# Adding x by a GpSimd transfer instead of VectorE, with GpSimd in the recorded order and a margin on ScalarE

## The chip, the cores and the metric

The kernel runs on one core of a Trainium2 chip. The metric is the device time of one execution in microseconds (us). Before the change the median of three runs is 2365.49 us (2364.38 to 2368.03).

The engines go by the profile's names: PE is TensorE's matrix multiplication and PEld its weight load, DVE is VectorE, ACT is ScalarE, POOL is GpSimd, SP is the engine that issues most transfers. Each runs its own queue of instructions in order; semaphores tie them together.

## The reference

Two graph layers on x (64 samples of 256 nodes by 256 features), both with the same matrix `adj` (256 by 256) and a residual:

```python
def reference(x, adj, L0_W1, L0_W2, L0_W3, L1_W1, L1_b1, L1_W2, L1_b2):
    # layer 0
    G = adj * adj
    h = maximum(layernorm(x), 0)
    h = relu(G @ (h @ W1)); h = relu(G @ (h @ W2))   # 256 -> 512 -> 1024
    x = x + G @ (h @ W3)                             # 1024 -> 256
    # layer 1
    h = maximum(layernorm(x), 0)
    U = eigenvectors of the normalized Laplacian of adj (jnp.linalg.eigh)
    x = x + U @ (relu((U.T @ h) @ W1 + b1) @ W2 + b2)
```

Layer 0 needs only `adj`. Layer 1 needs the eigenvectors, which are found on the chip.

## The kernel before

**Two kinds of work beside each other.** The class `Eigen` finds U in one long chain of dependent small steps: 254 Householder steps (`tridiagonalize`), small blocks (`leaves`), four levels of merging (`level`, 32 to 256), and two last products (`vectors`, `join`). VectorE does most of it; TensorE gives short transposes and products, ScalarE squares and roots, GpSimd powers and one-element steps. The class `Layers` does the two layers on 32 pairs of samples. Each pair's tiles have 128 partitions: [P, H, 2, N] is 128 partitions by two halves of the nodes by two samples by 256 features, 512 KB in f32.

**The order.** `Pace` puts both into one program. The chain's instructions are issued as they are written (`Pace.chain`). Each `Op` has an estimated busy time, and `Pace` keeps a clock for each engine and for each tile. Before it issues an instruction of the chain, `run` issues instructions of the streams (the layers' work) for as long as `fits` says that they can be done before the chain's is due. An instruction that is due sits at `ready` plus `LATER` (0.4 us for TensorE, 0.1 us for ScalarE). Ahead of a chain instruction on TensorE a stream's instruction need only start before that (0.5 us later for ScalarE's); ahead of one on another engine a stream's TensorE or ScalarE instruction has to end before it, and a stream's instruction of the remaining engines need only start. Large products can be cut at the limit (`Op.cut`). Until U is done, `manual_schedule` (L2352) keeps the recorded order for TensorE and ScalarE; the order of VectorE, GpSimd and SP in that stretch comes from the library's own scheduler. In the layer-1 stretch (`layer1`) all engines keep the recorded order.

**The streams.** `products` (L1905) holds the matrix work of layer 0. In the round of pair q it does the third product of q (`third_by_seven`, seven products for eight; its ScalarE copies and two adding transfers from GpSimd, `add`, fill tile s2), in it the rows of the pair before (`last(q - 1)`), then the first product and the widening of pair q+1, `rectify`, then `turn_rows` (transposes of the normalized rows of pair q-1 on TensorE), `fourth`, and `for_layer1(q - 1)`, which forms hw and spills it to DRAM. `rows` (L1950) holds the norms: `begin(q + 2)` loads x and normalizes it for layer 0, then, when `last(q)` is done (`q in self.new`), `norm1(q)` normalizes x1 in place for layer 1. `turn_rows` waits until `norm1` has been issued.

**x1.** There is one tile `x1`. Before, `products` loads x of pair q into it by two transfers on SP, after `for_layer1(q - 1)` has read the tile for the last time. In `last(q)` TensorE forms G p3 in a PSUM bank, for m = 0 and 1, and VectorE adds the bank onto x1 (128x512 each). After m = 1 the tile is spilled to DRAM by SP for layer 1's residual, and `norm1` begins: four sums and four squares on ScalarE (`norm`), three small steps on GpSimd (v, scale by a power, shift), four relu on ScalarE (`relu_norm`).

**The chain's ScalarE and GpSimd steps.** In a Householder step of the first half (lo < 128) `below` squares and sums the new row xr on ScalarE (tile tail, shown as m) and copies one element on GpSimd; `length` forms nn on VectorE, its root s0 by a power on GpSimd and the sign q on GpSimd. nb (shown as m<-q,s) needs s0 and q. The tile none on GpSimd needs tail and nn and is read by den. The transposes of ac and of a column of A (psB, psA) are TensorE's part. In the second half the root is ScalarE's. In `level` the roots rdq and the powers zh and rn are GpSimd's.

In the profile nearly every instruction has line L208, that of the recorder's call; tiles tell them apart: x<-x,bank is the add onto x1, bank<-eye,x is `turn_rows`, bank<-p,gt is `last`, bank<-hw,u and bank<-ut,s belong to layer 1, psA<-q,m is a chain product at the end of a level.

Of the kernel before, what the change touches and what calls it, by code (L numbers as in the profile page):

```python
# [21 lines left out]
F32 = mybir.dt.float32  # L22
AF = mybir.ActivationFunctionType
OP = mybir.AluOpType
# [135 lines left out]
class Pace:  # L160
# [9 lines left out]
    LEAD = 1.5  # L170

    def __init__(self, nc):
        self.slower, self.lead, self.no_haste = self.SLOWER, 0.0, False
        self.now = Proxy(nc, self.chain)
        self.later = Proxy(nc, lambda op: op)
        self.clock = dict.fromkeys(ENGINES.values(), 0.0)
        self.written, self.read, self.streams, self.on = {}, {}, [], True
# [32 lines left out]
    def chain(self, op):  # L210
        if not self.on:
            return op.call(*op.args, **op.kwargs)
        due = self.ready(op) + self.LATER.get(op.engine, 0.0)
        if self.no_haste:
            due = max(due, self.clock[op.engine] + 0.01)
        self.run(due, None if self.no_haste else op.engine)
        return self.issue(op, self.slower)

    def fits(self, op, start, limit, engine):
        if engine is None or op.engine not in ("PE", "ACT"):  # L220
            return start < limit
        if engine == "PE":
            return start < limit + self.HOP * (op.engine == "ACT")
        return start + op.busy + self.lead * (op.engine == "ACT") < limit
# [55 lines left out]
class Eigen:  # L280
# [162 lines left out]
    def tridiagonalize(self, a):  # L443
# [63 lines left out]
        for k in range(N - 2):  # L507
            lo = k + 1
            r, rest = slice(lo, N), slice(lo + 1, N)
            halves = [0, 1] if lo < P else [1]  # L510
            hs = slice(halves[0], H)
            rc = a[:, :, lo]

            nb = nbs[:, k : k + 1]
            if qn is not None:
                rs, qs = self.col("rs", 1), self.col("qs", 1)
                self.recip(rs, s0)
                self.tt(qs, q, s0, OP.mult)
            xa, junk = self.col("xa"), self.row("r0")
            for h in halves:  # L520
                self.stt(junk[:, r], a[:, h, r], 1.0, xr[:, r], OP.mult, OP.mult, accum=xa[:, h : h + 1])
                if h == halves[0] and qn is not None:
                    self.stt(nb, rs, qn, qs, OP.mult, OP.add)
            if qn is None:
                self.stt(nb, q, 2.0, s0, OP.mult, OP.mult)

            ac, uc = self.col("ac"), us[:, :, k]
            self.stt(ac[:, hs], rc[:, hs], nb, xa[:, hs], OP.mult, OP.add)
            pu, pr = as_row("psB", ac, halves), as_row("psA", rc, halves)

            none = self.col("none", 1)
            nc.gpsimd.tensor_scalar(none, tail, 1e-30, 1e30, OP.is_le, OP.mult)
            nc.gpsimd.tensor_tensor(none, none, nn, OP.add)
            den, gg, gu = (self.col(c, 1) for c in ("den", "gg", "gu"))
            gam = gams[:, k : k + 1]
            u1 = xr[:, lo : lo + 1]
            self.tt(u1, u1, nb, OP.add)
            self.stt(den, alpha, nb, none, OP.mult, OP.add)
            self.recip(gam, den)
            self.stt(uc, ident[:, :, lo], nb, xc, OP.mult, OP.add)  # L540
            aside(lo).tensor_tensor(gg, gam, gam, OP.mult)
            aside(lo).tensor_tensor(gu, gg, u1, OP.mult)
            gc, gr = self.col("gc"), row("gr")
            if halves[0]:
                self.tt(gc[:, hs], ac[:, hs], gam, OP.mult)
            else:
                self.ts(gc, ac, gam, OP.mult)

            uau, c = self.col("uau", 1), self.col("c", 1)
            self.stt(junk[:, r], pu[:, r], 1.0, xr[:, r], OP.mult, OP.mult, accum=uau)  # L550
            self.ts(gr[:, r], pu[:, r], gam, OP.mult)

            xn, xcn, both, f = row("xr"), self.col("xc"), self.row("r1"), self.col("f", 1)
            self.stt(both[:, rest], gr[:, rest], u1, pr[:, rest], OP.mult, OP.subtract)
            self.stt(f, uau, gu, gr[:, lo : lo + 1], OP.mult, OP.subtract)
            self.stt(xn[:, rest], xr[:, rest], f, both[:, rest], OP.mult, OP.subtract)
            more = lo + 1 < N - 1
            if more:
                alpha1, tail1 = below(xn, lo + 1)
            self.stt(c, uau, 0.5, gg, OP.mult, OP.mult)  # L560
            wr, wc = row("wr"), self.col("wc")
            self.stt(wr[:, r], xr[:, r], c, gr[:, r], OP.mult, OP.subtract)
            self.stt(wc[:, hs], uc[:, hs], c, gc[:, hs], OP.mult, OP.subtract)
            if more and halves[0]:
                following = length(xn, lo + 1, tail1)
            if halves[0]:
                nc.gpsimd.memset(xcn[:, 0:1], 0.0)
            self.stt(xcn[:, hs], gc[:, hs], u1, rc[:, hs], OP.mult, OP.subtract)
            self.stt(xcn[:, hs], uc[:, hs], f, xcn[:, hs], OP.mult, OP.subtract)
            aside(lo).tensor_tensor(xcn[:, hs], xcn[:, hs], self.lower[:, hs, lo], OP.mult)  # L570
            if more and not halves[0]:
                following = length(xn, lo + 1, tail1)

            for h in halves:
                self.stt(a[:, h, r], wr[:, r], uc[:, h : h + 1], a[:, h, r], OP.mult, OP.add)
                self.stt(a[:, h, r], xr[:, r], wc[:, h : h + 1], a[:, h, r], OP.mult, OP.add)
            xr, xc = xn, xcn
            if more:
                alpha, tail, (nn, s0, q, qn) = alpha1, tail1, following

        done = slice(0, N - 2)
        e0 = self.row("r1")[:, done]
        self.tt(e0, nbs[:, done], alphas[:, done], OP.add)
# [1186 lines left out]
class Layers:  # L1770
# [46 lines left out]

    def load(self, q):
        self.x = x = self.io.tile([P, H, 2, N], F32, tag="x", name="x")
        rows = self.view(self.ap["x"], q)  # L1820
        for i in range(2):
            at = (slice(None), slice(None), i) if q == 0 else (slice(None), i)
            yield self.nc.sync.dma_start(out=x[at], in_=rows[at])
# [81 lines left out]
    def products(self):  # L1905
# [3 lines left out]
        for q in range(PAIRS):  # L1909
            more, seven = q + 1 < PAIRS, q >= SEVEN_FROM  # L1910
            if q == SEVEN_FROM:
                yield from self.fold_weights()
            last = self.last(q - 1) if q > 0 else iter(())
            for part in self.third_by_seven() if seven else self.third():
                if part is None:
                    yield from next(last, ())
                else:
                    yield part
            if more:
                yield from self.first(q + 1)  # L1920
                for b in range(2):
                    yield from self.widened(b)
            if seven:
                yield from self.rectify(0)
            forms = iter(())
            if more:
                forms = self.spread_by_seven() if q + 1 >= SEVEN_FROM else self.spread_in_turn()
            if q > 0:
                yield lambda: q - 1 in self.h1
                yield from self.turn_rows()  # L1930
            yield from next(forms, ())
            if seven:
                yield from self.rectify(1)
            products = self.fourth()
            yield from next(products)
            if q > 0:
                yield from self.for_layer1(q - 1)
            for i in range(2):
                yield self.nc.sync.dma_start(out=self.x1[:, i], in_=self.view(self.ap["x"], q)[:, i])
            for part in products:  # L1940
                yield from next(forms, ())
                yield from part
# [7 lines left out]
    def rows(self):  # L1950

        yield from self.begin(0)
        for q in range(PAIRS):
            for p in [1, 2] if q == 0 else [q + 2]:
                if p < PAIRS:
                    yield lambda: p - 1 in self.begun
                    yield from self.begin(p)
            yield lambda: q in self.new
            yield from self.norm1(q)

    def begin(self, q):
# [219 lines left out]
    def last(self, q):  # L2181

        nc, x1 = self.nc, self.x1
        def rows(m):
# [1 line left out]
            yield from self.products_of(  # L2186
                ps, [(self.gt2[:, h, m * P : (m + 1) * P], self.p3[:, h, :]) for h in range(H)]
            )
            yield nc.vector.tensor_tensor(flat(x1)[:, m, :], flat(x1)[:, m, :], ps, OP.add)
            if m == H - 1:  # L2190
                yield nc.sync.dma_start(out=self.spilled[q], in_=x1.rearrange("p h b f -> p (h b f)"))
                self.new.add(q)

        for m in range(H):
# [138 lines left out]
def tile_kernel(ctx: ExitStack, tc: tile.TileContext, ap):  # L2333
# [5 lines left out]
    with ExitStack() as inner:  # L2339
# [9 lines left out]

        layers.nc, layers.now = pace.later, pace.now  # L2350
        pace.streams = layers.streams()
        with tc.manual_schedule(engines={mybir.EngineType.PE, mybir.EngineType.Activation}):  # L2352
            eigen.vectors(u, ut)
            pace.go_on(FLAG_US)
        pace.on = False
# [37 lines left out]
```

## Time and profile before

| what | value |
|---|---|
| median of the runs | 2365.49 us |
| the profiled execution, its own time | 2369.36 us |
| its span | 2367.6 us |
| TensorE idle in the span (span less busy) | 77.4 us |
| VectorE, x<-x,bank | 64 instructions, 43.4 us |
| ScalarE busy | 1183.8 us |
| GpSimd busy | 698.7 us |
| loads of x by SP (into x and into x1) | 128 transfers of 256 KB, 3.0 us to landing |
| adding transfers by GpSimd | 93 of 768 KB, 5.8 to 5.9 us to landing |

A line of the page's groups reads: line, engine, operation, out<-in by tile names, shape, count; then busy time in all and mean ns of one; then idle time of the engine before these and what ended it. A line of the waits reads: engine, what it was about to write, what it waited for, then us in all, times, the longest. A line of a timeline reads: start and duration in us, engine, line, operation, out<-in, count, and in brackets the idle time before and its releaser; equal neighbours are merged. A line of the stretches gives the window, its length, the busy time of PE, PEld, DVE, ACT and POOL with counts, the clock granted to TensorE as a share of full speed, the share of the transfer engines, and GB/s. A 128x256 product in f32 is two instructions in the profile.

### The profile page before, as it was taken

The numbers are of one execution on the slowest core, as the hardware profiler recorded it, in microseconds if no ns is written. First come the engines' busy times: TensorE is split into PE (matmuls) and PEld (weight loads), VectorE is DVE, ScalarE is ACT, GpSimd is POOL, SyncE is SP. The second block draws the span as 40 slices with busy tenths as digits, with TensorE's granted clock in tenths as the row PEclk, the third lists the DMA queues.
The fourth block names the chain that finished last, engine by engine and source line by source line (L and its number), as shares of the span: only waits on it lengthen the run. The fifth ranks groups of instructions, "written<-read, shape, count | busy, mean of one in ns | idle before, by whom it ended". The sixth has DMA issues, their size and how long they took to land. (4 is left out here: it accounts for less than half of the span.)

```text
span 2367.6 us, 40804 instructions
## 1 busy us (share of the span) xinstructions
PE 2290.2 (97%) x10652; PEld 1854.7 (78%) x10652; DVE 2005.0 (85%) x12072; ACT 1183.8 (50%) x2951; POOL 698.7 (30%) x1946
## 2 busy tenths in 40 slices
PE   7999999999999999999999899999999999999999
PEld 4687878787777877787888788777778777887888
DVE  7999999999999999999999899999877687882343
ACT  4455554555555555555555345555554455543322
POOL 3444544445554222222222001111111111111443
PEclk9999999999999999999999999999999999999999
DMA  4022222122222222222222222322322222223675
GB/s 134 23 70 61 65 57 70 51 69 63 59 59 62 72 56 61 69 67 59 72 63 60 58 63 72 72 72 59 72 63 63 59 58 72 54 63 103 217 251 203
DMA packets 91359, 183.26 MB, mean 77 GB/s; under 512 B 8432, under 2 KB 61808, under 8 KB 91120
## 3 DMA queue, kind: packets, MB, share of 16 engines
q0 software_dynamic: 13392, 73.14, 15.6%
q1 hardware_dynamic: 77728, 107.45, 13.4%
q8 instruction: 86, 1.41, 0.2%
q14 instruction: 153, 1.25, 0.2%
HBM read 65.48 MB, written 41.94 MB: 45 GB/s over the span
## 5 line engine op out<-in xcount | busy, mean ns | idle before, releaser
L208 PE MATMUL bank<-forms,L_gnn_W 128*128 128x256 f32 (+2 forms) x2102 | 490.7, 382 | 9.2 <-DVE x L208 6.1
L208 PE MATMUL bank<-L_gnn_W,s 128*128 128x256 f32 x2086 | 476.0, 378 | 4.8 <-ACT s L208 4.7
L208 PEld LDWEIGHTS bank<-forms,L_gnn_W 128*128 128x128 f32 x2102 | 390.6, 191 | 73.3 <-issue 11.7
L208 PEld LDWEIGHTS bank<-L_gnn_W,s 128*128 128x128 f32 x2086 | 391.7, 192 | 57.3 <-ACT s L208 5.7
L208 ACT ACTIVATE s<-bank 128x512 f32<-128x512 f32 (+1 forms) x485 | 278.7, 579 | 174.3 <-PE bank L208 173.3
L208 PE MATMUL bank<-forms,sums 128*128 128x256 f32 (+1 forms) x1512 | 347.0, 377 | 0.0
L208 PEld LDWEIGHTS bank<-forms,sums 128*128 128x128 f32 x1512 | 283.3, 191 | 53.4 <-issue 15.5
L208 PE MATMUL bank<-gt,s 128*128 128x256 f32 (+1 forms) x1036 | 246.3, 377 | 1.1 <-ACT s L208 1.1
L208 PE MATMUL bank<-L_gnn_W,y 128*128 128x512 f32 (+3 forms) x538 | 230.8, 572 | 1.1 <-ACT y L208 1.1
L208 ACT ACTIVATE forms<-bank 128x512 f32<-128x512 f32 x217 | 128.9, 594 | 180.9 <-PE bank L208 180.7
L208 PEld LDWEIGHTS bank<-gt,s 128*128 128x128 f32 x1036 | 188.9, 190 | 24.8 <-ACT s L208 2.6
L208 POOL COPY m<-xr 128x1 f32<-128x1 f32 x254 | 59.9, 236 | 418.1 <-DVE xr L208 418.0
L208 PEld LDWEIGHTS bank<-L_gnn_W,y 128*128 128x128 f32 x538 | 98.7, 190 | 98.2 <-issue 87.3
L208 ACT ACTIVATE junk<-xr 128x254 f32<-128x254 f32 (+63 forms) x127 | 46.0, 362 | 200.5 <-DVE xr L208 200.4
L208 ACT ACTIVATE junk<-x 128x256 f32<-128x256 f32 x256 | 105.8, 413 | 71.9 <-issue 44.0
L208 DVE SCALAR_TENSOR_TENSOR A<-xr,wc,A 128x255 f32<-128x255 f32 (+63 forms) x381 | 139.2, 368 | 0.0
L208 DVE SCALAR_TENSOR_TENSOR A<-wr,q,A 128x255 f32<-128x255 f32 (+63 forms) x381 | 138.0, 365 | 0.0
L208 ACT ACTIVATE junk<-x,nm 128x256 f32<-128x256 f32 x256 | 128.7, 503 | 4.0
L208 PE MATMUL bank<-p,gt 128*128 128x512 f32 (+2 forms) x272 | 122.8, 567 | 0.0
L208 PE MATMUL bank<-gt,h 128*128 128x256 f32 (+1 forms) x520 | 119.1, 379 | 0.1
L208 DVE SCALAR_TENSOR_TENSOR r<-A,xr 128x255 f32<-128x255 f32 (+63 forms) x381 | 117.8, 309 | 0.2
L208 PE MATMUL psB<-ident,ac 128*128 128x128 f32 x381 | 84.7, 277 | 27.2 <-DVE z L208 15.0
(614 smaller groups left out, 4639.5 us busy)
## 6 DMA issues: line engine op xcount, KB each, us to landing
x<-in_x_dram SPq DMA_DIRECT2D x128, 256.0 KB, 3.0
x<-x SPq DMA_DIRECT2D x64, 512.0 KB, 3.5
forms<-forms POOLq DMA_DIRECT2D x31, 768.0 KB, 5.8
s<-s POOLq DMA_DIRECT2D x31, 768.0 KB, 5.9
s<-forms POOLq DMA_DIRECT2D x31, 768.0 KB, 5.8
hw<-hw SPq DMA_DIRECT2D x64, 256.0 KB, 3.1
out_dram<-out SPq DMA_DIRECT2D x64, 256.0 KB, 2.2
L_gnn_W<-in_L_gnn_W_dram SPq DMA_DIRECT2D x1, 2048.0 KB, 11.2
```

Of the source, the lines that this page charges most:

```text
L208: return op.call(*op.args, **op.kwargs)
```

## The change

1. `Pace` gets `late`, which is added to the due time of the chain's ScalarE instructions. `tridiagonalize` sets it to 0.5 us in the steps of the first half and 0.2 us in those of the second, and to 0 after them.
2. `fits` has a rule for GpSimd: ahead of a GpSimd instruction of the chain, a stream's GpSimd instruction goes only when it ends before the limit. `manual_schedule` now covers GpSimd as well, so its queue keeps the recorded order until U is done.
3. `last` copies the bank into x1 by ScalarE. The two loads of x into x1 go. In `rows`, before `norm1`, GpSimd issues a transfer that adds x from DRAM onto x1 (512 KB), and the spill by SP follows it there.
4. The host lays x out by tile, [pair, partition, half, sample, feature], so that a partition's part of a pair is contiguous in DRAM. `load` reads it in this form.

```diff
@@ -170,7 +170,7 @@
     LEAD = 1.5
 
     def __init__(self, nc):
-        self.slower, self.lead, self.no_haste = self.SLOWER, 0.0, False
+        self.slower, self.lead, self.no_haste, self.late = self.SLOWER, 0.0, False, 0.0
         self.now = Proxy(nc, self.chain)
         self.later = Proxy(nc, lambda op: op)
         self.clock = dict.fromkeys(ENGINES.values(), 0.0)
@@ -210,13 +210,15 @@
     def chain(self, op):
         if not self.on:
             return op.call(*op.args, **op.kwargs)
-        due = self.ready(op) + self.LATER.get(op.engine, 0.0)
+        due = self.ready(op) + self.LATER.get(op.engine, 0.0) + self.late * (op.engine == "ACT")
         if self.no_haste:
             due = max(due, self.clock[op.engine] + 0.01)
         self.run(due, None if self.no_haste else op.engine)
         return self.issue(op, self.slower)
 
     def fits(self, op, start, limit, engine):
+        if engine == "POOL" == op.engine:
+            return start + op.busy < limit
         if engine is None or op.engine not in ("PE", "ACT"):
             return start < limit
         if engine == "PE":
@@ -509,6 +511,7 @@
             r, rest = slice(lo, N), slice(lo + 1, N)
             halves = [0, 1] if lo < P else [1]
             hs = slice(halves[0], H)
+            self.pace.late = 0.5 if lo < P else 0.2
             rc = a[:, :, lo]
 
             nb = nbs[:, k : k + 1]
@@ -578,6 +581,7 @@
             if more:
                 alpha, tail, (nn, s0, q, qn) = alpha1, tail1, following
 
+        self.pace.late = 0.0
         done = slice(0, N - 2)
         e0 = self.row("r1")[:, done]
         self.tt(e0, nbs[:, done], alphas[:, done], OP.add)
@@ -1817,7 +1821,7 @@
 
     def load(self, q):
         self.x = x = self.io.tile([P, H, 2, N], F32, tag="x", name="x")
-        rows = self.view(self.ap["x"], q)
+        rows = self.ap["x"][q]
         for i in range(2):
             at = (slice(None), slice(None), i) if q == 0 else (slice(None), i)
             yield self.nc.sync.dma_start(out=x[at], in_=rows[at])
@@ -1935,8 +1939,6 @@
             yield from next(products)
             if q > 0:
                 yield from self.for_layer1(q - 1)
-            for i in range(2):
-                yield self.nc.sync.dma_start(out=self.x1[:, i], in_=self.view(self.ap["x"], q)[:, i])
             for part in products:
                 yield from next(forms, ())
                 yield from part
@@ -1956,6 +1958,8 @@
                     yield lambda: p - 1 in self.begun
                     yield from self.begin(p)
             yield lambda: q in self.new
+            yield self.nc.gpsimd.dma_start(out=self.x1, in_=self.ap["x"][q], accum_op=OP.add)
+            yield self.nc.sync.dma_start(out=self.spilled[q], in_=self.x1.rearrange("p h b f -> p (h b f)"))
             yield from self.norm1(q)
 
     def begin(self, q):
@@ -2186,9 +2190,8 @@
             yield from self.products_of(
                 ps, [(self.gt2[:, h, m * P : (m + 1) * P], self.p3[:, h, :]) for h in range(H)]
             )
-            yield nc.vector.tensor_tensor(flat(x1)[:, m, :], flat(x1)[:, m, :], ps, OP.add)
+            yield nc.scalar.copy(flat(x1)[:, m, :], ps)
             if m == H - 1:
-                yield nc.sync.dma_start(out=self.spilled[q], in_=x1.rearrange("p h b f -> p (h b f)"))
                 self.new.add(q)
 
         for m in range(H):
@@ -2349,7 +2352,7 @@
 
         layers.nc, layers.now = pace.later, pace.now
         pace.streams = layers.streams()
-        with tc.manual_schedule(engines={mybir.EngineType.PE, mybir.EngineType.Activation}):
+        with tc.manual_schedule(engines={mybir.EngineType.PE, mybir.EngineType.Activation, mybir.EngineType.Pool}):
             eigen.vectors(u, ut)
             pace.go_on(FLAG_US)
         pace.on = False
@@ -2378,6 +2381,7 @@
 
     nc = bacc.Bacc("TRN2", target_bir_lowering=False, num_devices=1)
     data = {name: np.ascontiguousarray(inputs[name]) for name in INS}
+    data["x"] = data["x"].reshape(PAIRS, 2, H, P, N).transpose(0, 3, 2, 1, 4).copy()
     data.update(constants())
     arrays, ap = {}, {}
     for name, a in data.items():
@@ -2385,7 +2389,7 @@
         ap[name] = nc.dram_tensor(
             f"in_{name}_dram", a.shape, mybir.dt.from_np(a.dtype), kind="ExternalInput"
         ).ap()
-    ap["out"] = nc.dram_tensor("out_0_dram", data["x"].shape, F32, kind="ExternalOutput").ap()
+    ap["out"] = nc.dram_tensor("out_0_dram", inputs["x"].shape, F32, kind="ExternalOutput").ap()
     with tile.TileContext(nc) as tc:
         tile_kernel(tc, ap)
     r = run_bass_kernel_spmd(nc, [arrays], core_ids=[0])
```

## The prediction

> **What bounds the kernel now.** I read the page first, then the waits of TensorE, then the stretches and timelines in which it stood still.
>
> ```profile
> span 2367.6 us, 40804 instructions
> PE 2290.2 (97%) x10652; PEld 1854.7 (78%) x10652; DVE 2005.0 (85%) x12072; ACT 1183.8 (50%) x2951; POOL 698.7 (30%) x1946
> ```
>
> TensorE is the bound: 2290.2 of 2367.6 us busy, so 77.4 us of idle time. The eigenvalue chain (mostly VectorE) runs beside the layers until about 2178 us and takes small slots of TensorE. A faster chain alone therefore gains nothing; only time in which TensorE stands still, or runs slowly, can be won. The waits of TensorE name it:
>
> ```profile
> PE psB L208 <- DVE z L208: 15.0, 19, 1.9
> PE psB L208 <- DVE xr L208: 10.6, 12, 1.7
> PE bank L208 <- ACT s L208: 8.6, 6, 3.8
> ...
> PE bank L208 <- DVE x L208: 6.1, 5, 3.6
> PE psA L208 <- DVE m L208: 4.8, 1, 4.8
> ```
>
> The first two are the tridiagonalization (transposes that came before the chain was ready), the others single stalls later. Two of those, at the chain's end:
>
> ```profile
> 2152.49 1.04 PE L208 MATMUL bank<-eye,x 128*128 128x128 f32 x8
> 2158.35 3.78 PE L208 MATMUL psA<-q,m 128*128 128x256 f32 x8 [4.82 <-DVE m L208]
> 2161.93 4.46 PE L208 MATMUL bank<-L_gnn_W,s 128*128 128x256 f32 x14
> ...
> 2194.39 3.02 PE L208 MATMUL bank<-ut,s 128*128 128x256 f32 x8 [2.80 <-ACT s L208]
> ```
>
> A stall costs more than its idle time. In dense stretches 16 of the 128x256 instructions start within 3.46 us (2149.03 to 2152.49), 0.216 us each. After the 4.82 us of idle time the next 22 took from 2158.35 to 2166.22, 7.87 us instead of 22 x 0.216 = 4.75: 3.1 us more. The stretches show why: the granted clock.
>
> ```profile
> 2158.00:2162.00 4.00, 3.65 (x9) 2.93 (x10) 0.69 (x2) 1.06 (x1) 0.00 (x0) 0.50 0.16 32
> 2162.00:2166.00 4.00, 4.00 (x14) 3.29 (x13) 0.88 (x2) 1.47 (x5) 0.70 (x1) 0.69 0.00 0
> ```
>
> (The last three figures are clock, DMA share and GB/s.) The same dip, 0.50 and then about 0.7, follows the stalls at 1769.61 (3.76 us), 1878.49 (3.61 us) and 2194.39 (2.80 us). I price each at 3.1 us on top of the stall. The Trainium skill (TensorE: Matmul & The Clock Gate, Part 1) halves the clock only after an idle window of about 3.4 us and for about 3.4 us. By it the 2.80 us stall would be free of a dip and the other three would cost some 1.7 us each, 5.1 us in all, an estimate; the rows give four dips and 12.4 us, and I go by the rows.
>
> **The adds leave VectorE.** Removed are 64 adds from PSUM; added are 64 ScalarE copies and 32 adding transfers issued by GpSimd.
>
> ```profile
> L208 DVE TENSOR_TENSOR x<-x,bank 128x512 f32<-128x512 f32 x64 | 43.4, 680 | 19.2 <-PE bank L208 19.2
> L208 ACT COPY x<-bank 128x512 f32<-128x512 f32 x64 | 34.4, 579 | 2.4 <-PE bank L208 2.3
> ```
>
> VectorE loses 43.4 us of work and 19.2 us of standing before a bank. ScalarE gains 64 x 0.579 = 37 us on an engine half idle. For TensorE the direct effect is that a bank is emptied by a short copy and not by an add behind the chain's instructions: the 6.1 us of waits for "DVE x" go, and the dip after the 3.61 us one: 6.1 + 3.1 = **-9.2 us**. Cover gone would mean the same wait for the copy instead (+9 us). I add **+1** for 64 more bank releases by ScalarE.
>
> **The path of x1.** Before, the last normalized rows (relu) stood 8.6 to 11.9 us after the second add, and in all but the last two pairs TensorE turned them only 24 to 32 us after the add. Now the copy (0.58) is followed by an issue on GpSimd (the existing adding transfers take 0.97 us on the queue) and a landing; 768 KB of that kind land in 5.8 to 5.9 us. 512 KB aren't in the trace: between the 3.0 us of a plain 256 KB load and 5.9 us; I take 5.9, the same kind. The path grows by 0.58 + 0.97 + 5.9 - 0.68 = 6.8 us, to 15.4 to 18.7 us, inside the 24 us. It costs nothing, hidden by the rest of the third product, the first product and the widening of the next pair; without that cover it would be 6.8 us a pair. The spill waits for the landing and must be read before the relu overwrites x1, but means, squares and GpSimd's three steps (at least 6 us) still lie between; on SP's queue only later loads and spills of hw stand behind it, a pair (66 us) ahead. SP also loses 64 loads into x1, which nobody waited for. The layout by tile turns 1 KB runs into 2 KB on loads hidden anyway. The Trainium skill (SBUF — State Buffer, SBUF: two separate sides) speaks against a transfer issued by GpSimd beside a busy VectorE: from 0.62 to 3.1 us in its example, an estimated 2.5 us a pair. The 31 transfers of tile s here landed in 5.7 to 6.9 us with VectorE 94% busy, and 2.5 us more would still be hidden.
>
> **Tridiagonalization (50 to 1310 us).** Here 36 of the adds lay in VectorE's chain: 36 x 0.68 = 24.5 us, and one 4.1 us wait. Against it stands ScalarE's margin of 0.5 us (first half of the steps) and 0.2 us. In the trace the chain's Square begins within 0.094 us of its row in 124 of 127 steps, and VectorE's nn starts 0.033 us after the total: no slack, so a filler in the way delays VectorE in full. Bounds: 0 and 127 x 0.5 + 127 x 0.2 = 89 us. ScalarE is about 55% busy, so I take half the steps, delayed by half the margin: 127 x 0.125 + 127 x 0.05 = 22 us. GpSimd now has its power before the sign and "none": s0 ends about 0.5 us sooner, but nb also needs the sign (0.46 us), so nothing is won or lost. The chain gains 28.6 - 22 = 6.6 us. The built programs' orders agree: priced at 0.432 us per 256-column product, step 240 stands behind 1277.9 us of TensorE work instead of 1285.1. Chain and order move together, so the waits stay: **0**, between -15 (most of the 24 us idle here) and +22 (the delay is double).
>
> **GpSimd by the clock.** The queue's order now comes from the recorder. What that mends is this:
>
> ```profile
> 1764.14 0.72 POOL L208 TENSOR_TENSOR rdq<-rdq,half 128x2 f32<-128x2 f32 x1 [4.36 <-DVE rdq L208]
> ...
> 1766.30 0.20 POOL L208 TENSOR_TENSOR shift<-nm,scale 128x4 f32<-128x4 f32 x1
> ```
>
> The layers' norm waited behind a root of the chain that waited 4.36 us for VectorE; ScalarE's relu waited for the shift, its rectification for the relu, TensorE 3.76 us for that, plus the dip. I credit this 3.8 + 3.1 and the two smaller "ACT s" waits after 1400 us with 0.9 + 0.3, at seven in ten: **-6 us**; such meetings may also arise anew (bounds -8 and +7). At the start the power of the degrees no longer stands behind the norm's three (11.89 us, ready at 10.70): **-1 us**.
>
> **The chain's end.** Total matrix work is the same: 5957 instead of 5960 products in the built program. But the last product of the chain stands behind 2169.3 us of TensorE work instead of 2187.5. So 18 us of layer 0 are left to lie beside the chain's last waits and the first layer-1 pairs: between the transposes of the last level and psA<-q,m there are now some 10.5 us of products instead of 5.2. Idle there was 4.8 + 2.8 + 0.5 + 0.5 = 8.6 us and two dips 6.2: 14.8. The last pair keeps a short path: 31 products, 13.4 us, between its second copy and its turning, against 15.4: 2 us. **-12 us**, bounds -14.8 and -4.
>
> Sum: -9.2 + 1 + 0 - 6 - 1 - 12 = -27; I keep 2 us for new meetings on ScalarE: **-25 us**, a span of 2343 for 2367.6. The profiled execution itself took 2369.4 us, 3.9 above the median of 2365.5; the same difference on the median gives **2341 us**.
>
> **Rivals.** (A) The gain is given back: the margin delays the chain by 40 us rather than 22 while the order expects 22, so the transposes wait some 18 us more, and one dip stays: 2341 + 21 = 2362. For it: nn has no slack. Against: the order contains the margin already. (B) Slower: GpSimd's queue blocks the chain. Each adding transfer waits in order for a ScalarE copy; the chain's power, sign and "none" stand behind it, and psB with them. It decides from a lateness of 0.15 us in each of 254 steps, 38 us: 2341 + 38 = 2379. For it: "m" on VectorE already follows the power by 0.033 us in the median. Against: only 20 pairs meet that half, and the new rule lets in only GpSimd work that ends before the chain's is due. (C) The waits of the tridiagonalization fall too, by 15 to 20 us: 2324. For it: VectorE loses its 4.1 us stall and GpSimd's collisions (12.9 us of "m" waiting for s).
>
> **Numbers.** Forecast 0.68 (own range 2330 to 2355), C 0.14, A 0.09, B 0.09. A measurement here tells some 0.2% (4.7 us) from no change. Faster: forecast and C, 0.82; within: A, 0.09; slower: B, 0.09. The range 2320 to 2364 leaves out B, half of A and a little of C.
>
> **What would show it.** Right: "DVE x" gone from TensorE's waits; psB waits near 25 us; no dip at 1880 and 2160; the last chain product some 18 to 25 us sooner; ScalarE busy about 1220 us, VectorE 1960. Wrong: TensorE waiting for "ACT x" at the turning of rows in every pair (the landing is not hidden), or psB waits over 45 us (A or B), with VectorE waiting for GpSimd's s, q or none if it is B.

## The result, and the profile after

The changed kernel takes 2385.2 us (median of 4 runs, 2384.4 to 2386.5) against 2366.4 us for the kernel before (2364.4 to 2368.0). The ratio is 1.008, with a 95% interval of 1.0063 to 1.0098: slower. The forecast was 2341 us and its range ended at 2364: the time moved the other way.

The head of the page after, from the profiled execution:

```profile
span 2384.7 us, 40670 instructions
PE 2292.4 (96%) x10646; PEld 1850.6 (78%) x10646; DVE 1975.8 (83%) x12008; ACT 1227.1 (51%) x3015; POOL 723.7 (30%) x1978
```

TensorE is as busy as before to 2 us and the span is 17.1 us longer, so TensorE still bounds the kernel and stands idle for longer. VectorE has 29 us less work, and the kernel gained nothing by it. The waits of TensorE after (total us, number, longest):

```profile
PE psB L208 <- DVE z L208: 32.8, 31, 3.2
PE psB L208 <- DVE xr L208: 20.1, 29, 1.6
PE bank L208 <- ACT s L208: 5.6, 5, 4.4
...
PE bank L208 <- DMA hw<-hw: 3.9, 1, 3.9
```

"DVE x" is gone, as the change meant. But the two psB rows, the transposes of the tridiagonalization that find their operand not ready, went from 25.6 us in 31 waits to 52.9 us in 60. What VectorE waited for in that stage shows why. Between 50 and 1310 us, before:

```profile
DVE r L208 <- PE psB L208: 22.3, 74, 1.0
DVE m L208 <- POOL s L208: 10.0, 30, 1.1
...
DVE den L208 <- POOL none L208: 3.6, 12, 0.6
```

and after:

```profile
DVE r L208 <- PE psB L208: 36.3, 58, 3.6
DVE den L208 <- POOL none L208: 34.0, 50, 1.9
DVE m L208 <- POOL q L208: 9.7, 16, 1.7
DVE nn L208 <- ACT junk L208: 2.1, 6, 0.8
```

The new wait is den's, for GpSimd's none: 3.6 us became 34.0 us. ScalarE's margin, which the prediction counted as a cost, shows in the last row as 2.1 us of waiting. One such step (n = 153) in the timeline after. GpSimd:

```profile
649.55 0.38 POOL L208 COPY m<-xr 128x1 f32<-128x1 f32 x1
649.90 0.55 POOL L208 TENSOR_TENSOR xc<-xc,lower 128x2 f32<-128x2 f32 x1
650.41 1.20 POOL L208 TENSOR_TENSOR scale<-v,rsqrt 128x4 f32<-128x4 f32 x1
651.59 0.53 POOL L208 TENSOR_TENSOR s<-nn,half 128x1 f32<-128x1 f32 x1
652.10 0.22 POOL L208 TENSOR_SCALAR q<-xr 128x1 f32<-128x1 f32 x1
652.30 0.19 POOL L208 TENSOR_TENSOR shift<-nm,scale 128x4 f32<-128x4 f32 x1
652.57 0.27 POOL L208 TENSOR_SCALAR none<-m 128x1 f32<-128x1 f32 x1
652.92 0.19 POOL L208 TENSOR_TENSOR none<-none,nn 128x1 f32<-128x1 f32 x1
```

and VectorE in the same step:

```profile
652.35 0.16 DVE L208 SCALAR_TENSOR_TENSOR m<-q,s 128x1 f32<-128x1 f32 x1 [1.65 <-POOL q L208]
...
653.14 0.22 DVE L208 SCALAR_TENSOR_TENSOR den<-m,none 128x1 f32<-128x1 f32 x1 [0.40 <-POOL none L208]
```

and TensorE:

```profile
649.66 1.04 PE L208 MATMUL bank<-eye,x 128*128 128x128 f32 x8
653.64 0.40 PE L208 MATMUL psB<-ident,ac 128*128 128x128 f32 x2 [2.95 <-DVE z L208]
```

VectorE's nn was ready at 649.6 us, but GpSimd took the layers' scale (1.20 us) ahead of the power s, and their shift between the sign q and none. VectorE stood 1.65 + 0.40 us, z came late, and TensorE, whose order is fixed, stood 2.95 us before the transpose. Layers' work (the norm's v, scale and shift, and the issues of transfers) stands between the copy of alpha and the none pair in 65 of 254 steps after, in 5 before. In the recorded program none comes late in a step, behind nb, ac and as_row, and the streams of the layers are recorded up to there as GpSimd's planned clock allows. The library's scheduler, which ordered GpSimd before, had almost always put none ahead of them. Between 50 and 1310 us den waits 41.8 us for none in the changed kernel, the waits too short for the view included: 15.9 us in steps with operations of the norm alone in between, 17.2 us in steps with the issue of a transfer, 8.8 us in steps with no layers' work there.

**One account for all kernels.** Take each TensorE product's start minus the start before it, less its dense pitch in the trace (216 ns for 256 columns, 429 for 512, 110 for 128, 323 for 384): the rest is time lost, idle or at a halved clock. In all 14 kernels of this study the span less that loss is 2264.4 to 2264.9 us. So every difference below is time that TensorE lost, and the place can be told: until the last row (xr) of the tridiagonalization, in the leaves and levels until the first product with the vectors (hw,u), and behind it. "Ahead" is the TensorE work that stands in the queue before that last row: the row's time less the loss until then (some 4.5 us of start-up are in it).

```
kernel                            time   lost: tridiag. levels end   last row  ahead
before                          2366.4           51.9   43.4   7.5   1299.7   1247.8
after                           2385.2           89.6   20.7   9.9   1330.9   1241.3
e1 GpSimd by library            2367.4           58.3   36.3   8.5   1299.6   1241.3
e2 no margin                    2395.3           91.6   28.5  11.8   1318.7   1227.1
e3 before, GpSimd by clock      2394.7           90.6   33.2   5.8   1338.1   1247.5
e4 none recorded early          2372.7           62.6   33.2  10.9   1293.3   1230.7
e5 x1 alone                     2384.9           65.9   42.3  12.0   1292.9   1227.0
e6 margin alone                 2377.2           61.7   40.7   8.7   1313.9   1252.2
e7 by clock behind only         2352.2           54.5   20.8   8.5   1295.8   1241.3
e8 e7 without margin            2372.4           65.4   27.7  12.4   1292.4   1227.0
e9 before, by clock behind only 2357.6           51.7   33.8   5.6   1299.2   1247.5
e10 e7, half margin             2369.0           58.0   32.8  11.1   1288.4   1230.4
e11 e5, copy on VectorE         2371.6           56.1   43.8   3.0   1303.7   1247.6
e12 e7, 1.5 x margin            2350.3           51.5   26.2   4.7   1310.9   1259.4
```

(us; times are medians, all else is from one profiled execution of each kernel. Beside e1 to e12 the kernel before took 2365.7 to 2367.5 us.) Up to the last row e1 and e7 run the same sequence on all five queues and still differ by 3.8 us, so differences of that size tell nothing. From before to after, the tridiagonalization lost 37.7 us and the levels won 22.7.

### The profile page after: what moved, and what is told of

Its sections match the earlier page's. It is cut to its first block, busy times and chain, and to the rows that moved or that the text cites. A ratio compares the mean times of both kernels' runs of the same rounds, so it can differ in the third digit from the quotient of the medians.

```text
span 2384.7 us, 40670 instructions
## 1 busy us (share of the span) xinstructions
PE 2292.4 (96%) x10646; PEld 1850.6 (78%) x10646; DVE 1975.8 (83%) x12008; ACT 1227.1 (51%) x3015; POOL 723.7 (30%) x1978
## 3 DMA queue, kind: packets, MB, share of 16 engines
q1 hardware_dynamic: 52384, 90.67, 10.9%
## 5 line engine op out<-in xcount | busy, mean ns | idle before, releaser
L208 PE MATMUL bank<-forms,L_gnn_W 128*128 128x256 f32 (+1 forms) x2098 | 489.0, 381 | 0.8 <-DVE ac L208 0.8
L208 PE MATMUL bank<-L_gnn_W,s 128*128 128x256 f32 (+1 forms) x2076 | 474.1, 378 | 5.3 <-ACT s L208 5.2
L208 PEld LDWEIGHTS bank<-gt,s 128*128 128x128 f32 x1046 | 193.9, 193 | 25.5 <-ACT s L208 1.8
L208 PE MATMUL psB<-ident,ac 128*128 128x128 f32 x381 | 85.9, 280 | 55.1 <-DVE z L208 32.8
L208 PEld LDWEIGHTS psB<-ident,ac 128*128 128x128 f32 x381 | 46.5, 136 | 109.4 <-issue 59.3
L208 PE MATMUL bank<-p,gt 128*128 128x512 f32 (+3 forms) x268 | 122.7, 573 | 0.0
L208 PE MATMUL bank<-gt,h 128*128 128x256 f32 x514 | 118.3, 380 | 0.0
```

## The experiments

**e1: GpSimd back to the library's order, the rest of the change kept.**

```diff
-with tc.manual_schedule(engines={PE, Activation, Pool}):
+with tc.manual_schedule(engines={PE, Activation}):
```

> The changed kernel with GpSimd's order left to the library's scheduler again, as it was before; margin, copy, adding transfer and layout stay. Theory 'late none': with GpSimd issued in the recorded order, work of the layers stands between a step's alpha and its none, because none is recorded last in the step; den waits for none, the chain slides, TensorE waits for psB. It expects 2340 us (2330 to 2350), VectorE's den waiting under 5 us for none (41.8 us in the changed kernel), TensorE's waits for psB released by z and xr near 25 us. Rival 'margin': the ScalarE margin makes nn wait; expects 2380 us (2370 to 2390), psB waits still over 45 us. Rival 'blocked queue': the adding transfer on GpSimd's queue waits for the copy and holds up the chain behind it; expects 2370 to 2385 us.

Measured: 2367.4 us, ratio 1.0004 (0.9994 to 1.0014). VectorE's waits between 50 and 1310 us:

```profile
DVE r L208 <- PE psB L208: 25.0, 64, 4.0
DVE m L208 <- POOL s L208: 13.7, 34, 1.8
DVE den L208 <- POOL none L208: 5.8, 10, 1.4
DVE nn L208 <- ACT junk L208: 4.7, 8, 1.0
```

den's wait falls to 5.8 us, and the psB waits to 30.4 us. The margin stayed and den's wait went: "margin" falls as the cause of the slowdown. But the time is that of before, not 2340: copy, transfer and margin together are worth nothing here, and the order of GpSimd had also won something in the levels (20.7 us lost with it, 36.3 without). Up to the last row TensorE, ScalarE and SP run the same sequence in e1 as in the changed kernel. GpSimd's differs, and VectorE's with it (1093 of 7548 places), since the library orders VectorE. What is measured here as the price of GpSimd's order includes this.

**e2: no margin.**

```diff
-self.pace.late = 0.5 if lo < P else 0.2
+self.pace.late = 0.0
```

> The changed kernel with the ScalarE margin set to 0 in all steps; GpSimd issued in the recorded order, copy, adding transfer and layout stay. Theory 'late none': 2385 us (2379 to 2391), den still waiting over 30 us for none. Rival 'margin': 2345 us (2335 to 2360). Rival 'blocked queue': 2385 us.

Measured: 2395.3 us, ratio 1.0117 (1.01 to 1.0134); den waits 36.4 us between 50 and 1310 us. Without the margin the kernel is 10 us slower, outside the interval of every theory, and the opposite of what "margin" says. The last row comes 12.2 us sooner, but 14.2 us less TensorE work stands ahead of it, and the levels lose 7.8 us more.

**e3: the kernel before, with nothing but GpSimd by the clock.**

```diff
-with tc.manual_schedule(engines={PE, Activation}):
+with tc.manual_schedule(engines={PE, Activation, Pool}):
...
 def fits(self, op, start, limit, engine):
+    if engine == "POOL" == op.engine:
+        return start + op.busy < limit
```

> The kernel before with only GpSimd issued in the recorded order by the planner's clock; x1 is still added by VectorE and loaded by SP, no margin. Theory 'late none': slower than before, 2400 us (2390 to 2415), den waiting 30 us or more for none. Rivals 'margin' and 'blocked queue', which need the margin or the adding transfer: 2366 us, den waiting for none as little as before (4 us).

Measured: 2394.7 us, ratio 1.0113 (1.0096 to 1.013), as "late none" expected. Between 50 and 1310 us:

```profile
DVE den L208 <- POOL none L208: 39.4, 53, 2.3
DVE r L208 <- PE psB L208: 25.5, 46, 2.0
```

The whole loss of the tridiagonalization is there (90.6 us against 89.6 after), without a copy on ScalarE, an adding transfer or a margin: GpSimd's order is the cause of it. The new rule in `fits` alone is not: e1 keeps it and loses 58.3 us. The rival "blocked queue" falls too, as far as it means the transfer of x (only 7 of the 65 steps have one ahead of none). The older adding transfers stand in GpSimd's queue in e3 as well, and their part isn't told apart from the norm's.

**e4: none recorded early.** All three parts of the change stay; the sign is recorded right behind alpha, the first none operation ahead of nn, the second behind the power.

```diff
 nc.gpsimd.tensor_copy(alpha, xr[:, lo : lo + 1])
+q = self.col("q", 1)
+if lo < P:
+    nc.gpsimd.tensor_scalar(q, xr[:, lo : lo + 1], 0.0, 0.5, OP.is_ge, OP.subtract)
...
+nc.gpsimd.tensor_scalar(none, tail, 1e-30, 1e30, OP.is_le, OP.mult)
 self.stt(nn, x1, x1, tail, OP.mult, OP.add)
 if lo < P:
     self.power(s0, nn, 0.5)
-    nc.gpsimd.tensor_scalar(q, x1, 0.0, 0.5, OP.is_ge, OP.subtract)
+    nc.gpsimd.tensor_tensor(none, none, nn, OP.add)
...
-nc.gpsimd.tensor_scalar(none, tail, 1e-30, 1e30, OP.is_le, OP.mult)
-nc.gpsimd.tensor_tensor(none, none, nn, OP.add)
```

> The changed kernel with the order of recording of three small GpSimd operations changed: the sign right behind alpha, and the none pair around the power instead of at the end of the step, so that none of the layers' operations can be put between them. All else of the change stays. Theory 'late none': 2340 us (2330 to 2350), den waiting under 8 us for none, psB waits near 25 us. Rival 'margin': 2380 us. Rival 'blocked queue': 2380 us, since copy, adding transfer and queue are the same.

Measured: 2372.7 us, ratio 1.0023 (1.0014 to 1.0033). VectorE between 50 and 1310 us:

```profile
DVE r L208 <- PE psB L208: 27.3, 73, 4.0
DVE m L208 <- POOL s L208: 18.3, 40, 1.4
DVE nn L208 <- ACT junk L208: 2.7, 5, 0.8
```

den's wait for none is gone and the last row comes 37.6 us sooner than in the changed kernel, by the order of recording alone: 27.0 us of it is lost time won back, the rest is less TensorE work ahead. The mechanism stands. The time still missed the 2340 us, for two reasons that the table shows. The recorder put 10.6 us less TensorE work ahead of the chain (1230.7 for 1241.3), presumably because it counts on a shorter step, and the psB waits were 35.6 us where 25 were expected. And the levels lost 33.2 us where the changed kernel lost 20.7. Behind 1400 us products waited 12.4 us for ScalarE's s, 4.7 us in the changed kernel. Why those meetings were worse here stays open.

**e5 and e6: x1 alone, the margin alone**, each on the kernel before with GpSimd by the library.

```diff
-yield nc.vector.tensor_tensor(flat(x1)[:, m, :], flat(x1)[:, m, :], ps, OP.add)
+yield nc.scalar.copy(flat(x1)[:, m, :], ps)
...
 yield lambda: q in self.new
+yield self.nc.gpsimd.dma_start(out=self.x1, in_=self.ap["x"][q], accum_op=OP.add)
+yield self.nc.sync.dma_start(out=self.spilled[q], in_=self.x1.rearrange("p h b f -> p (h b f)"))
```

> The kernel before with only x1 = x + G p3 moved: ScalarE copies the bank, the adding transfer on GpSimd's queue adds it to x laid out by tile, the spill is issued in the norms' stream. No margin, GpSimd ordered by the library. What is open is where the gain of taking the adds off VectorE went: with GpSimd by the library, margin and x1 together gave 2367 us, no change. Theory 'x1 pays': the bank waits for x vanish and the time falls to 2352 us (2345 to 2358); then the margin gives it back. Theory 'x1 gives it back': ScalarE, loaded with 28.6 us less spare time, makes steps late, psB waits rise by about 10 us; 2367 us (2362 to 2372).

> The kernel before with only the longer margin on ScalarE's chain operations in the steps (0.5 us, then 0.2 us). If the margin is what gave back the gain of x1: 2377 us (2371 to 2384). If the margin is neutral or helps: 2366 us (2358 to 2369).

Measured: x1 alone 2384.9 us, ratio 1.0077 (1.006 to 1.0094); margin alone 2377.2 us, 1.0045 (1.0028 to 1.0061). Together (e1) they cost nothing. Neither theory for e5 had 2385. e6 has the time of its first theory, but not for that reason: x1 alone had no gain that the margin could give back. The waits of TensorE in e5:

```profile
PE psB L208 <- DVE z L208: 24.4, 29, 2.5
PE psB L208 <- DVE xr L208: 12.9, 18, 1.6
PE bank L208 <- ACT s L208: 12.8, 9, 4.3
PE bank L208 <- ACT y L208: 7.3, 6, 3.1
PE bank L208 <- DMA x<-x: 7.0, 1, 7.0
```

With the adds off VectorE the recorder put 20.8 us less TensorE work ahead of the last row (1227.0 for 1247.8), but the chain came only 6.8 us sooner (1292.9 for 1299.7). The 14.0 us between are what the tridiagonalization lost more. Behind the levels e5 loses 4.5 us more than before; the last row of the view is the first product with the vectors, which stood until loads of layer 1 had landed. The margin makes the recorder expect a later chain: 14.3 us of work go back in front (1241.3 in e1), and the loss falls to 58.3 us. The rule in `fits`, which e1 has and e5 has not, moves nothing: e8 has it without the margin and stands at 1227.0 us like e5. Without x1 (e6) the margin puts only 4.4 us more work in front, and the loss rises by 9.8 us: the last row comes at 1313.9 us.

**e7: GpSimd by the library in the tridiagonalization, by the clock behind it.** Everything else is the changed kernel.

```diff
-with tc.manual_schedule(engines={PE, Activation, Pool}):
-    eigen.vectors(u, ut)
+engines = {PE, Activation}
+with tc.manual_schedule(engines=engines):
+    d, e, reflections = eigen.tridiagonal()
+with tc.manual_schedule(engines={*engines, Pool}):
+    eigen.vectors(u, ut, d, e, reflections)
```

> The changed kernel with GpSimd ordered by the library in the tridiagonalization and by the planner's clock only behind it (leaves, levels, vectors). If the two stages add up, TensorE loses 71 us up to 1400 us, as with GpSimd by the library throughout, and 19 us behind it, as in the changed kernel, so 2355 us (2348 to 2362): faster than both kernels. If the gain behind 1400 us came with the late tridiagonalization and not from GpSimd's order: 2367 us.

Measured: 2352.2 us, ratio 0.9947 (0.9931 to 0.9964): faster than both kernels. The head of its page and its first waits of TensorE:

```profile
span 2348.2 us, 40670 instructions
PE 2281.9 (97%) x10646; PEld 1850.5 (79%) x10646; DVE 1973.2 (84%) x12008; ACT 1227.4 (52%) x3015; POOL 734.8 (31%) x1978
```

```profile
PE psB L208 <- DVE z L208: 19.6, 26, 3.0
PE psB L208 <- DVE xr L208: 9.9, 12, 1.4
```

It has the same 1241.3 us of work ahead of the last row as the changed kernel, and the row comes at 1295.8 instead of 1330.9 us: the 35.1 us are the price of GpSimd's recorded order in the tridiagonalization (31.3 by e1, which has the same orders in this stage). The two stages add up as expected: 54.5 + 20.8 + 8.5.

**e8, e9, e10, e12: what that version owes to its parts.** e8 has late = 0.0, e10 late = 0.25 and 0.1, e12 late = 0.75 and 0.3 in place of 0.5 and 0.2. e9 is the kernel before with e3's fits and e7's two stages.

> The changed kernel with GpSimd by the library in the tridiagonalization and by the clock behind it, and with no margin. The margin was worth 18 us beside x1 with GpSimd by the library throughout (2367 against 2385 us), and cost 11 us without x1 (2377 against 2366 us). If it pays because ScalarE carries x1: 2370 us (2363 to 2377), the loss mostly before 1400 us. If the runs with and without it only differ by how the filler happens to fall behind 1400 us, which the clock order changes: 2352 us (2346 to 2359).

> The kernel before with GpSimd by the clock only behind the tridiagonalization; x1 added by VectorE, no margin. If GpSimd's order behind is the whole gain of that version: 2353 us (2347 to 2359), and x1 with its margin is worth nothing even there. If the copy, the adding transfer and the margin carry part of it: 2366 us (2360 to 2370), with VectorE's x still waited for.

> The changed kernel with GpSimd by the library in the tridiagonalization and by the clock behind it, and half the margin (0.25 us, then 0.1 us). If the time falls steadily with the margin: 2361 us, between the two. If there is a least value: 2352 us or below (2344 to 2356). If small shifts of the filler decide it: anywhere from 2345 to 2375 us, on neither line.

> The changed kernel with GpSimd by the library in the tridiagonalization and by the clock behind it, and a margin half as long again (0.75 us, then 0.3 us). Time by margin so far: none 2372, half 2369, whole 2352 us. If the margin works by keeping ScalarE's chain operations in time, and more of it still helps: 2345 us (2338 to 2351). If the whole margin is a lucky fit of the filler: 2362 us or more.

Measured: e8 2372.4 us (ratio 1.0019, 1.001 to 1.0029), e9 2357.6 us (0.9961, 0.9946 to 0.9975), e10 2369.0 us (1.0005, 0.9995 to 1.0014), e12 2350.3 us (0.9938, 0.9921 to 0.9954), the least of the study, though not told apart from e7. GpSimd by the clock behind the tridiagonalization is worth 10 us without x1 (e9, in the range of its first expectation) and 13 to 15 us with x1 and margin (e1 to e7, with and without the runs of before beside each). Of the gain of e7 the copy, the transfer and the margin carry 4 to 5 us, and only together: x1 without the margin is 15 us worse than without x1 (e8 against e9). e8 has the time of its first theory, but only 10.9 of its 21.7 us more loss than e7 lie in the tridiagonalization. e10 lies on neither line; its third theory had so wide a range that a hit says little. e12 lies where more margin still helps. In the tridiagonalization the loss falls with the margin, 65.4, 58.0, 54.5 and 51.5 us, as more work stands ahead, 1227.0, 1230.4, 1241.3 and 1259.4 us. The last three differ from their neighbours by less than the 3.8 us between e1 and e7, the first by more. The levels follow no such line (27.7, 32.8, 20.8, 26.2), and the time falls by only 3.4 us for the first half of the margin and by 16.8 for the second, so it is no steady function of the margin.

**e11: x1 alone, with the copy on VectorE.**

```diff
-yield nc.scalar.copy(flat(x1)[:, m, :], ps)
+yield nc.vector.tensor_copy(flat(x1)[:, m, :], ps)
```

> The version with x1 alone (2385 us against 2366 us before), with the copy of the bank made by VectorE instead of ScalarE; the adding transfer, the spill in the norms' stream and the layout stay, no margin, GpSimd by the library. If ScalarE's added copies are what made steps and levels late: 2366 us (2360 to 2371), the stalls before 1300 us falling from 66 to near 52 us. If the adding transfer on GpSimd's queue, or the moved spill, is what costs: 2385 us (2379 to 2391).

Measured: 2371.6 us, ratio 1.0025 (1.0015 to 1.0034), just outside both expectations. So about 14 of x1's 19 us are in the copy's move to ScalarE, and the transfer, spill and layout cost the other 5. That the copies on ScalarE make it late isn't shown by this: with the copy on VectorE the recorder also put the work back in front (1247.6 us), which e5's account explains as well.

## Why the prediction was wrong, step by step

- **"GpSimd now has its power before the sign and none ... nothing is won or lost", and with it the 0 for the tridiagonalization (bounds -15 and +22).** This is the step that failed. It weighed the chain's own operations against each other and not the layers' work that may now stand between them. Against rival B it held that the new rule lets in only work that ends before the chain's is due; that is so in the planned clock, not on the chip, where the layers' scale (1.20 us) stood ahead of the power at 650 us. Measured: 37.7 us more lost; 31 to 35 us of it by GpSimd's order (e1 and e7 to after), the other 3 to 6 us by x1 and the margin. The upper bound held ScalarE's delay only.
- **"Chain and order move together, so the waits stay".** It failed as well. The order moved 6.5 us forward, as the built programs said (7.2); the chain moved 31.2 us back. In e5 they moved 20.8 and 6.8 us. Taking the recorder's order as a witness for the chain's speed was the error: that order is only what its planned times say.
- **The margin as a cost of 22 us to the chain.** nn waits 2.1 us for ScalarE in the changed kernel. The last row does come later with the margin than without it, by 3.4 to 12.2 us beside x1 (e8 to e7, e5 to e1, e2 to after) and by 14.2 us alone (e6); how much of that is ScalarE's delay and how much the work put in front isn't shown. For the kernel's time the sign was wrong: taking the margin away costs 10 to 20 us where x1 is on ScalarE (e2, e5, e8). It costs 11 us where x1 is not (e6). Rival A falls.
- **Adds off VectorE, -9.2 + 1.** The "DVE x" waits went. In e1, where GpSimd's order doesn't interfere, waits for ScalarE's y (6.2 us after 1400 us) came in their place: from the last row to the transposes of the last level e1 lost 35.8 us, 34.4 before. Nothing was won.
- **The path of x1 hidden.** Right: 512 KB land in 5.4 us (5.9 taken), and no product waited for them at the turning of rows (ACT x: 1.3 us in all). The sum of the path counted the issue's 0.97 us twice, since the time to landing runs from the start of the issue (tile s before: 5.86 us from its start, 4.89 from its end).
- **GpSimd by the clock, -6.** Right in sign and place and too small: 10 to 15 us behind the tridiagonalization, against a bound of -8. The stall at 1770 us went; one of 4.4 us at 1493 us came.
- **The chain's end, -12.** The order left 17 us more TensorE work for it (18 predicted), and psA<-q,m no longer waits. But the first product with the vectors then waited 3.9 us for hw, plus a dip. From the last level's transposes on 16.5 us were lost before and 10.4 after: the end won 6 us, half of what was predicted.
- **Rival B** named the right engine and the right witness, VectorE waiting for none. Its mechanism, the adding transfer that waits for a copy, was not it: e3 has none and loses the same. In the changed kernel GpSimd does stand 25.7 us before such transfers between 50 and 1290 us, but the loss is no greater than in e3.

- **Rival C** had the psB waits fall by 15 to 20 us. They doubled.

By the account the change lost 37.7 us more in the tridiagonalization (0 predicted), 1.4 more in the levels by x1 and the margin (e1; -8.2 predicted), 15.6 less there by GpSimd's order (e1 to after; -6 predicted) and 6.1 less at the chain's end (-12 predicted). That is +17.4 us beside the 17.1 by which the span grew.

## What to carry to other kernels

Taking an engine's order out of a scheduler's hands binds it to the order in which the program happens to be recorded: look first for what is recorded late and needed early, and for what may then be put before it. Hand over one stage at a time, since the same order here won in one stage and lost twice as much in another. Where one engine's queue is laid out by a planned clock, time that the plan believes saved and the chip doesn't save can return as waits of that engine (e5): compare how far the plan moved with how far the chain did.

## What the hardware showed unexpectedly

The granted clock halves after short idle times of TensorE also in the tridiagonalization, where the trace of before had none. After, around the stall of 4.4 us that ends at 1493 us (clock is the third figure from the end):

```profile
1488.00:1492.00 4.00, 0.96 (x5) 0.97 0.00 0
1492.00:1496.00 4.00, 2.65 (x6) 0.50 0.40 131
1496.00:1500.00 4.00, 4.00 (x16) 0.68 0.00 0
```

The dips of this trace last 3.41 us (behind the psB waits at 150, 434 and 580 us, of 2.40 to 3.24 us) or twice that (behind the stalls at 1493 and 2179 us). Not every stall brings one: that of 2.95 us at 653 us had none. All four dips of before lasted 6.83 us, one of them behind 2.80 us of idle time. So a late transpose can cost more than its wait, which the psB rows don't show: behind the one at 150 us the products start up to 0.43 us apart instead of 0.216, 1.7 us in all. The Trainium skill (TensorE: Matmul & The Clock Gate, Part 1) has the clock halved after an idle window of about 3.4 us; the length of the short dips agrees, the dips behind 2.80 and 2.40 us of idle time don't.
